# First sequence's norm taken on rows, its K in a second PSUM bank, passes for the clock, later transposes, and V's copies on ScalarE

## The chip, the cores and the metric

The kernel runs on one core of one Trainium2 chip. The metric is the device time in microseconds, as the median of several executions. The engines are PE (TensorE), DVE (VectorE), ACT (ScalarE), POOL (GpSimd) and SP (SyncE, which only issues transfers here). [...]

## What is computed

x has 4 sequences of 512 tokens and 128 channels, all in float32. Two blocks follow each other, each on a layer norm and with a residual:

```
x = x + attention(layernorm(x))     # 16 heads of 64, S = 512
x = x + six_layers(layernorm(x))    # depth 6, windows of 32
```

The first block, in which the whole change lies:

```
q, k, v = x @ Wq, x @ Wk, x @ Wv            # 128 -> 16 heads x 64
scores = q . k / 8 - 50 * (key after query)  # a penalty, not a mask
out = softmax(scores) @ v @ Wr
```

The layer norm has no weights here: `(x - mean) / sqrt(var + 1e-5)` over the 128 channels of a token. The second block has six layers of windowed attention with normalised and rotated q and k, and a gated feed-forward; the change does not touch it.

## The kernel before

**Staging.** The kernel has two stages. The first stage (about 0 to 560 us) computes the first block, the second (to the end) the six layers. The order of all instructions on every engine is written out by hand; each engine takes them in the order of the source, apart from some transfers on SP.

**Layout.** x is loaded per sequence as `xr[b]`, with tokens in the partitions (128 rows, 4 tiles of 128 channels). `load_x` (L196 to L201) transposes the four tiles on PE into one PSUM bank (`pt_bank`, two buffers), and ACT copies them to `x0T[b]`, channels in the partitions and the 512 tokens along the free axis. `xr` has two buffers, so sequences 2 and 3 are loaded into the tiles of 0 and 1 once those were read. `xnT[b]` is the normed sequence in the same layout as `x0T`.

**The norm** (`layernorm_steps`, three steps) works on the transposed layout. `mean` multiplies by a matrix of 1/128 on PE (L94), subtracts on DVE (L96) and squares on ACT (L98). `var` sums the squares with four small products (L103), and DVE, or POOL for the later sequences, takes the inverse root by three Newton steps of four instructions (`rsqrt`, L80 to L86). `scale` spreads the result over the partitions with four transposes (L111) and multiplies (L115). For sequence 0 the steps stand in front of everything, with the transposes of all four sequences between them:

```
load_x(0); mean(); load_x(1); var(); load_x(2); load_x(3); scale()
make_q(0, 0)(); make_k(0, 0)
```

**Slots.** The rest of the first stage is a loop of 64 slots m, each with two tiles of 128 queries for a pair of heads c of a sequence b: `b, c, odd = m // 16, m // 2 % 8, m % 2`. In a slot PE computes the scores of two tiles (`scores`, L252) and adds the penalty (L267), DVE takes the row maxima (`maximum`, L279, and L281 for the columns that are all penalised), ACT the exponents with their sums (L290), DVE the inverse sums (L300, L301), POOL multiplies by them (`normalise`, L304). The products of the slot before, `old`, are transposed by PE (L315) and copied out by ACT (L319) and DVE (L323). `times_v1` (L335) multiplies older ones with V. An even slot computes the next pair's Q (`make_q`, L215, copied by ACT at L217), an odd one its K (`make_k`, L221, copied by DVE at L223).

**V** is computed by `make_v` (L231), one tile of 128 tokens for 8 heads at a time, copied by DVE at L238. There are 32 such copies of 128x512: two in slot 0, three in slot 1, and one in most odd slots.

**Banks.** Q, K, V, the steps of the norm and the output projection all use one PSUM bank, `bank1` with one buffer: each of these products waits until the copy of the one before has read it. `tmp` and `small` are pools in SBUF.

**Order on DVE in a slot:** the maximum of the first tile with its bias (L279, L281), V's copy if there is one, a step of the next sequence's norm if there is one, the copy at L323, the maximum of the second tile, K's copy in odd slots, then the sums and the second L323.

**Transfers.** SP issues the x loads, the constants and the second stage's weights; ACT's queue issues Wq, Wk and Wv at the start.

## Time and profile before

| what | value |
|---|---|
| median of 3 runs | 2278.62 us (2278.29 to 2281.74) |
| profiled execution: its time, and its span | 2281.5 us, 2279.7 us |
| PE busy | 2178.0 us (96%), 35088 instructions |
| DVE busy | 1729.1 us (76%), 2800 instructions |
| ACT busy | 1347.6 us (59%), 2550 instructions |
| POOL busy | 1451.3 us (64%), 1981 instructions |
| start of the first score product | 26.97 us |
| V's copy on DVE (L238) | 32 of 0.68 us |
| a copy of the same shape on ACT (L319) | 128 of 0.59 us |

In a line of the timeline the first number is the start in us from the first instruction, the second how long the group took; then engine, line of the source, operation, output<-input with shapes, and the count. A bracket tells how long the engine stood idle before it and what released it. PE counts a float32 product as two instructions. PEld is PE's loading of weights, which overlaps its products. The granted clock is the share of TensorE's full clock.

### The profile page before, as it was taken

Reading aid. Unit: us, or ns where it says so; the run is one execution under the profiler, and the core shown is the slowest. Engines: PE = TensorE matmul, PEld = TensorE weight load, DVE = VectorE, ACT = ScalarE, POOL = GpSimd, SP = SyncE. Lnnn points to the kernel's source line nnn. Section 1 sums busy time; section 2 is a strip of 40 time slices with the busy share of each in tenths; the row PEclk is TensorE's granted clock in tenths of the full one; section 3 lists DMA queues with packets and bytes.
Section 4 is the critical chain, followed back from the end, with each engine's and each line's share of the span. In section 5 each row is a group of like instructions: output and inputs, shape, how many; then the busy total and the mean of one; then the engine's idle time right before and its main releaser. Section 6 shows DMA issues by size and latency. Waiting matters only on the chain.

```text
span 2279.7 us, 82205 instructions
## 1 busy us (share of the span) xinstructions
PE 2178.0 (96%) x35088; PEld 1435.6 (63%) x35088; DVE 1729.1 (76%) x2800; ACT 1347.6 (59%) x2550; POOL 1451.3 (64%) x1981
## 2 busy tenths in 40 slices
PE   6999999999999999999999999999999999999997
PEld 3555555555566666666666666666666666666664
DVE  3776667767778787878887788878888878888774
ACT  3665655655455656666566666666656666666562
POOL 1544545455877677767677777677776667766760
PEclk8999999999999999999999999999999999999998
DMA  3000000000322233232322323222332223222220
GB/s 115 1 1 1 1 1 1 1 1 1 75 70 64 63 88 75 58 75 68 87 67 64 77 70 91 64 62 69 85 85 56 72 63 88 73 67 70 65 56 15
DMA packets 91029, 125.74 MB, mean 55 GB/s; under 512 B 25390, under 2 KB 39468, under 8 KB 90668
## 3 DMA queue, kind: packets, MB, share of 16 engines
q1 hardware_dynamic: 90236, 118.92, 21.1%
q8 instruction: 279, 4.57, 0.9%
q10 hardware_dynamic: 432, 1.57, 0.2%
q14 instruction: 82, 0.67, 0.1%
HBM read 20.31 MB, written 1.05 MB: 9 GB/s over the span
## 4 chain that ended last, share of the span: by engine, by line
PE 63%; DVE 9%; issue 2%; ACT 1%; POOL 0%; POOLq 0%; ACTq 0%
PE ps_proj L477 19%; PE ps_one L585 14%; PE ps_one L680 7%; PE ps_att L655 6%; PE ps_att L623 6%; PE ps_proj L713 3%; PE ps_proj L714 3%; PE ps_proj L727 2%; DVE yt L80 2%; DVE t L502 1%; DVE rot L498 1%; PE ps_att L612 1%; PE ps_one L94 1%; PE ps_one L103 1%; DVE yt L83 1%
## 5 line engine op out<-in xcount | busy, mean ns | idle before, releaser
L513 POOL TENSOR_TENSOR rot<-rot,t 128x1024 f32<-128x1024 f32 x192 | 453.8, 2364 | 197.5 <-DVE t L502 185.9
L477 PE MATMUL ps_proj<-wqkv,xs 128*128 128x512 f32 x1152 | 553.3, 603 | 4.3 <-DVE t L502 2.8
L304 POOL TENSOR_TENSOR pr<-pr,den 128x1024 f32<-128x1024 f32 x128 | 240.9, 1893 | 266.9 <-DVE den L301 258.6
L488 ACT ACTIVATE sq<-ps_proj 128x1024 f32<-128x1024 f32 x192 | 196.8, 1025 | 356.7 <-PE ps_proj L477 324.5
L521 POOL TENSOR_TENSOR rot<-rot,ss 128x1024 f32<-128x1024 f32 x192 | 365.2, 1902 | 14.9
L477 PEld LDWEIGHTS ps_proj<-wqkv,xs 128*128 128x128 f32 x1152 | 198.1, 190 | 166.1 <-issue 146.5
L493 DVE TENSOR_REDUCE ss<-sq 128x16 f32<-128x1024 f32 x192 | 233.1, 1214 | 46.9 <-ACT sq L488 46.3
L498 DVE TENSOR_TENSOR rot<-ps_proj,lt 128x1024 f32<-128x1024 f32 x192 | 233.6, 1217 | 0.0
L502 DVE TENSOR_TENSOR t<-ps_proj,lt 128x1024 f32<-128x1024 f32 x192 | 233.2, 1215 | 0.4 <-POOL rot L513 0.4
L290 ACT ACTIVATE pr<-ps_sc,nm 128x128 f32<-128x128 f32 (+3 forms) x448 | 220.1, 507 | 20.0 <-DVE nm L279 16.7
L279 DVE TENSOR_REDUCE nm<-ps_sc 128x2 f32<-128x1024 f32 x128 | 156.0, 1219 | 91.0 <-PE ps_sc L267 91.0
L585 PE MATMUL ps_one<-ident,rot 128*128 128x128 f32 x1536 | 211.3, 280 | 5.9 <-issue 4.4
L680 PEld LDWEIGHTS ps_one<-aT,wo 128*128 128x128 f32 x1536 | 186.3, 192 | 45.3 <-issue 44.5
L83 POOL TENSOR_TENSOR yt<-y 128x32 f32<-128x32 f32 (+1 forms) x309 | 72.9, 236 | 210.5 <-DVE y L81 194.3
L633 DVE TENSOR_REDUCE mx<-ps_att 128x16 f32<-128x1024 f32 x96 | 117.5, 1224 | 102.3 <-PE ps_att L623 102.2
L680 PE MATMUL ps_one<-aT,wo 128*128 128x128 f32 x1536 | 187.3, 275 | 0.4 <-ACT aT L588 0.4
L585 PEld LDWEIGHTS ps_one<-ident,rot 128*128 128x128 f32 x1536 | 165.3, 141 | 25.3 <-issue 7.1
L319 ACT COPY pT<-ps_pt 128x512 f32<-128x512 f32 x128 | 75.5, 590 | 176.2 <-PE ps_pt L315 176.2
L655 PEld LDWEIGHTS ps_att<-vw,pT 64*32 64x32 f32 x9216 | 103.5, 105 | 93.4 <-ACT pT L588 54.0
L567 ACT COPY vt<-ps_proj 128x512 f32<-128x512 f32 x192 | 103.2, 590 | 93.6 <-PE ps_proj L477 91.6
L315 PEld LDWEIGHTS ps_pt<-ident,pr 128*128 128x128 f32 x1024 | 117.6, 142 | 56.7 <-issue 47.6
L655 PE MATMUL ps_att<-vw,pT 64*32 64x65 f32 x9216 | 129.0, 225 | 24.2 <-DVE t L502 13.4
(134 smaller groups left out, 4062.3 us busy)
## 6 DMA issues: line engine op xcount, KB each, us to landing
vw<-vt SPq DMA_DIRECT2D x1152, 65.0 KB
vw_first<-vt SPq DMA_DIRECT2D x336, 65.0 KB
wqkv<-in_wqkv_dram SPq DMA_DIRECT2D x18, 512.0 KB
wo<-in_wo_dram SPq DMA_DIRECT2D x6, 512.0 KB
w<-in_w_dram SPq DMA_DIRECT2D x6, 341.0 KB
xr<-in_x_dram SPq DMA_DIRECT2D x4, 256.0 KB
out_dram<-tmp_t SPq DMA_DIRECT2D x4, 256.0 KB
w<-in_w_dram SPq DMA_DIRECT2D x12, 64.0 KB
```

What stands on the lines that cost most here:

```text
L290: nc.scalar.activation(self.pr[:, h, cols], self.sc[:, h, cols], AF.Exp, bias=self.nm[:, part_, h : h + 1], accum_out=self.den[:, part_, h ...
L304: nc.gpsimd.tensor_tensor(self.pr, self.pr, self.den[:, 0].unsqueeze(2).to_broadcast([P, 2, S]), ALU.mult)
L477: mm(p[:, c, :], lhsT=u.xs[:, u.T * P : (u.T + 1) * P], rhs=wpart[j][:, c * 512 : (c + 1) * 512], start=True, stop=True,)
L488: nc.scalar.activation(u.sq, u.p[j], AF.Square)
L493: nc.vector.tensor_reduce(u.ss[:, j * HEADS : (j + 1) * HEADS], heads(u.sq), AX.X, ALU.add)
L498: nc.vector.tensor_tensor(heads(t0), heads(pf), lt[:, u.T, 2 * j].unsqueeze(1).to_broadcast([P, HEADS, HD]), ALU.mult)
L502: nc.vector.tensor_tensor(t1.rearrange("p (h t d) -> p h t d", t=2, d=half), pf.rearrange("p (h t d) -> p h t d", t=2, d=half)[:, :, ::-1, :],
L513: nc.gpsimd.tensor_tensor(u.r[j], u.r[j], u.t1, ALU.add)
L521: nc.gpsimd.tensor_tensor(heads(u.r[j]), heads(u.r[j]), u.ss[:, j * HEADS : (j + 1) * HEADS].unsqueeze(2).to_broadcast([P, HEADS, HD]), AL ...
L585: nc.tensor.transpose(tp[:, c * P : (c + 1) * P], src[:, (4 * g + c) * P : (4 * g + c + 1) * P], ident)
L655: mm(o[j * W : (j + 1) * W, h, c * (HD + 1) : (c + 1) * (HD + 1)], lhsT=u.pT[h * HD : (h + 1) * HD, 4 * g + c, j * W : (j + 1) * W], rhs=u ...
L680: mm(y[:, 0:P], lhsT=wo_w[0][:, c, :], rhs=u.aT[:, c, :], start=(c == 0), stop=(c == NC - 1))
```

## The change

The change has five parts.

- **x of sequence 0 in halves.** SP loads tiles 0 and 1, ACT's queue loads tiles 2 and 3, ahead of Wq, Wk and Wv.
- **First norm on rows.** `first_norm` replaces the three steps for sequence 0. DVE takes mean and variance of each token from `xr[0]` with `bn_stats` and `bn_aggr` (four each), adds eps, takes the inverse root as before, and scales the four tiles; each is then transposed by PE, and ACT copies the four to `xnT[0]`. `load_x(0)` remains, for the residual. Sequence 1's transposes stand between the statistics and the new transposes.
- **Passes for the clock.** `warm(n)` issues n products that nobody reads: ten of 128x128 at the very start, and sixteen of 24 columns between sequence 1's transposes and the new ones.
- **K's bank.** The first K goes to a bank of `pt_bank`, the first Q stays in `bank1`. `load_x(2)` and `load_x(3)` move to the end of slots 2 and 3.
- **V's copies on ACT**, all 32. With it the bias of the maxima is a method of its own (`bias`), and the first tile's stands after the norm step instead of ahead of it.

```diff
--- before.py
+++ after.py
@@ -174,8 +174,12 @@
         pen = s1.tile([P, P], BF16, tag="pen", name="pen")
         xr = [s1.tile([P, NT, EMB], F32, tag="xr", name=f"xr{b}", bufs=2) for b in range(B)]
         for b in range(B):
-            nc.sync.dma_start(out=xr[b], in_=x[b].rearrange("(t p) e -> p t e", p=P))
-            if b == 0:
+            src = x[b].rearrange("(t p) e -> p t e", p=P)
+            if b:
+                nc.sync.dma_start(out=xr[b], in_=src)
+            else:
+                nc.sync.dma_start(out=xr[b][:, 0:2], in_=src[:, 0:2])
+                nc.scalar.dma_start(out=xr[b][:, 2:NT], in_=src[:, 2:NT])
                 nc.sync.dma_start(out=ident16, in_=a["ident16"])
                 nc.sync.dma_start(out=pen, in_=a["pen"])
         for t_, n_ in ((wq, "wq"), (wk, "wk"), (wv, "wv")):
@@ -205,7 +209,38 @@
                 xnT[b] = s1.tile([P, S], F32, tag="xnT", name="xnT", bufs=2)
                 return xnT[b]
 
-            return layernorm_steps({}, bank1, lambda: x0T[b], out_, eng=nc.gpsimd if b else nc.vector)
+            return layernorm_steps({}, bank1, lambda: x0T[b], out_, eng=nc.gpsimd)
+
+        def warm(n, rhs=avg):
+
+            p = bank1()
+            for _ in range(n):
+                mm(p[:, 0 : rhs.shape[1]], lhsT=avg, rhs=rhs, start=True, stop=True)
+
+        def first_norm():
+
+            x_ = xr[0]
+            raw = small.tile([P, NT, 6], F32, tag="bnst", name="bnst", bufs=1)
+            mv = small.tile([P, NT, 2], F32, tag="bnmv", name="bnmv", bufs=1)
+            for t in range(NT):
+                nc.vector.bn_stats(raw[:, t, :], x_[:, t, :])
+            for t in range(NT):
+                nc.vector.bn_aggr(mv[:, t, :], raw[:, t, :])
+            rs = small.tile([P, NT], F32, tag="rs", name="rs")
+            nc.vector.tensor_scalar(rs, mv[:, :, 1], EPS, None, ALU.add)
+            load_x(1)
+            warm(16, raw.rearrange("p t k -> p (t k)"))
+            rsqrt(rs, NT, nc.vector)
+            h = tmpt()
+            tp = pt_bank()
+            for t in range(NT):
+                cols = slice(t * P, (t + 1) * P)
+                nc.vector.tensor_scalar(
+                    h[:, cols], x_[:, t, :], mv[:, t, 0:1], rs[:, t : t + 1], ALU.subtract, ALU.mult
+                )
+                nc.tensor.transpose(tp[:, cols], h[:, cols], ident)
+            xnT[0] = s1.tile([P, S], F32, tag="xnT", name="xnT", bufs=2)
+            nc.scalar.copy(xnT[0], tp)
 
 
         qs, ks, vs, pTs, os_, aTs = {}, {}, {}, {}, {}, {}
@@ -216,8 +251,8 @@
             q = qs[b, c] = s1.tile([P, S], F32, tag="q1", name="q1", bufs=2)
             return lambda: nc.scalar.activation(q, p, AF.Copy, scale=0.125)
 
-        def make_k(b, c):
-            p = bank1()
+        def make_k(b, c, p=None):
+            p = bank1() if p is None else p
             mm(p, lhsT=wk[:, c * P : (c + 1) * P], rhs=xnT[b], start=True, stop=True)
             k = ks[b, c] = s1.tile([P, S], F32, tag="k1", name="k1", bufs=2)
             nc.vector.tensor_copy(k, p)
@@ -235,7 +270,7 @@
                 start=True,
                 stop=True,
             )
-            nc.vector.tensor_copy(vs[b, j][:, t, :], p)
+            nc.scalar.copy(vs[b, j][:, t, :], p)
 
         class Rows:
 
@@ -277,6 +312,8 @@
                 sc = self.sc
                 self.nm = small.tile([P, 2, 2], F32, tag="nm", name="nm")
                 nc.vector.tensor_reduce(self.nm[:, 0], sc, AX.X, ALU.max, negate=True)
+
+            def bias(self):
                 if self.t + 1 < NT:
                     nc.vector.tensor_scalar(self.nm[:, 1], self.nm[:, 0], PEN, None, ALU.add)
 
@@ -353,16 +390,11 @@
 
         rows = [Rows(b, c, t) for b in range(B) for c in range(NC) for t in range(NT)]
         norms, norms1 = {}, {}
-        mean, var, scale = norm_x(0)
+        warm(10)
         load_x(0)
-        mean()
-        load_x(1)
-        var()
-        load_x(2)
-        load_x(3)
-        scale()
+        first_norm()
         make_q(0, 0)()
-        make_k(0, 0)
+        make_k(0, 0, pt_bank())
 
 
         last = len(rows) // 2
@@ -392,11 +424,14 @@
                 norms[b + 1][c - 1]()
             if b in range(1, B) and not odd and 4 <= c <= 6:
                 norms1[b - 1][c - 4]()
+            if now:
+                now[0].bias()
             if old:
                 old[0].transposes()
             if now:
                 now[0].exponents()
                 now[1].maximum()
+                now[1].bias()
 
             bn, cn = (b, c + 1) if c + 1 < NC else (b + 1, 0)
             copies = []
@@ -411,6 +446,8 @@
                 now[1].exponents()
             for f in copies:
                 f()
+            if m in (2, 3):
+                load_x(m)
             if now:
                 now[1].inverse()
                 now[1].normalise()
```

## Prediction

> **What bounds the kernel now.** I read the page first: PE is busy 96% of the span, and the chain that ended last is 63% PE. The change touches only the first stage (0 to 560 us) and its start, so the answers must come from the first microseconds, then from one repeating slot.

> First the timeline of the start, up to the first score matmul:

> ```profile
> 5.64 1.08 PE L199 MATMUL ps_pt<-ident,xr 128*128 128x128 f32 x4 [5.64 <-DMA xr<-in_x_dram]
> ...
> 7.40 2.07 PE L94 MATMUL ps_pj<-x0T,avg 128*128 128x512 f32 x2 [0.68 <-ACT x0T L201]
> ...
> 9.29 1.11 PE L199 MATMUL ps_pt<-ident,xr 128*128 128x128 f32 x4
> ...
> 14.79 0.16 DVE L86 TENSOR_TENSOR rs<-y,yt 128x4 f32<-128x4 f32 x1
> ...
> 15.96 1.09 PE L199 MATMUL ps_pt<-ident,xr 128*128 128x128 f32 x4 [3.99 <-DMA xr<-in_x_dram]
> ...
> 18.64 1.08 PE L199 MATMUL ps_pt<-ident,xr 128*128 128x128 f32 x4 [1.60 <-DMA xr<-in_x_dram]
> ...
> 19.52 1.06 PE L111 MATMUL ps_pj<-ident,rs 128*128 128x128 f32 x4
> ...
> 21.36 2.07 PE L215 MATMUL ps_pj<-xnT,wq 128*128 128x512 f32 x2 [0.78 <-DVE xnT L115]
> ...
> 24.11 2.08 PE L221 MATMUL ps_pj<-xnT,wk 128*128 128x512 f32 x2 [0.69 <-ACT q L217]
> ...
> 26.97 3.79 PE L252 MATMUL ps_sc<-k,q 64*128 64x256 f32 x16 [0.78 <-DVE k L223]
> ```

> The reader is to see that the inverse root is ready at 14.95, but PE, which works in order, stands behind the transposes of sequences 2 and 3 until 19.4: 4.4 us that the norm doesn't need. Q and K share one bank, so K's matmul waits for Q's copy. The first scores start at 26.97. Each 128x512 product takes 2.07 us here. Next, stretches of the same time; the columns after the stretch are PE, PEld, DVE, ACT and POOL busy, granted clock, DMA share and GB/s:

> ```profile
> 7.30:10.70 3.40, 3.01 (x6) 1.22 (x6) 0.69 (x1) 0.52 (x2) 0.00 (x0) 1.00 1.06 378
> 10.70:14.10 3.40, 1.05 (x8) 0.97 (x8) 1.75 (x11) 0.63 (x2) 0.00 (x0) 1.00 1.09 348
> 14.10:17.50 3.40, 1.09 (x4) 0.71 (x4) 0.71 (x5) 0.42 (x1) 0.00 (x0) 0.50 1.13 312
> ...
> 24.30:27.80 3.50, 2.72 (x6) 1.06 (x8) 0.69 (x1) 0.00 (x0) 0.00 (x0) 0.50 0.00 0
> 27.80:31.20 3.40, 3.40 (x19) 2.32 (x18) 0.08 (x1) 0.00 (x0) 0.00 (x0) 0.50 0.00 0
> 31.20:34.60 3.40, 2.14 (x5) 0.48 (x4) 2.15 (x4) 1.93 (x8) 0.00 (x0) 1.00 0.00 0
> ```

> The granted clock is half until 31.2, except 10.7 to 14.1. A stretch with PE busy 3.01 of 3.40 raised it, one of 2.72 did not, one of 1.05 dropped it. (The 1.00 before 10.7 is only a missing record: the 2.07 us product at 7.40 ran at half clock.)

> Then one odd slot of the steady part (its first score matmul at 164.09, the next slot's at 172.21):

> ```profile
> 166.26 1.08 PE L231 MATMUL ps_pj<-wv,xnT 128*128 128x512 f32 x2
> 166.34 1.22 DVE L279 TENSOR_REDUCE nm<-ps_sc 128x2 f32<-128x1024 f32 x1 [0.20 <-PE ps_sc L267]
> ...
> 167.68 0.68 DVE L238 COPY v<-ps_pj 128x512 f32<-128x512 f32 x1
> 167.81 0.59 ACT L319 COPY pT<-ps_pt 128x512 f32<-128x512 f32 x1 [2.08 <-PE ps_pt L315]
> ...
> 168.42 1.13 PE L221 MATMUL ps_pj<-xnT,wk 128*128 128x512 f32 x2 [0.21 <-DVE v L238]
> ```

> V's product ends at 167.34, but DVE is in the maximum until 167.56, so V's copy ends at 168.36, and K's product, which needs the same single bank, waits. ACT stood idle for 2.08 us up to 167.81. The waits of PE between 40 and 555 us say how often:

> ```profile
> PE ps_pj L221 <- DVE v L238: 8.5, 27, 0.6
> ```

> It is the largest of PE's waits in the stage. A plain slot without V takes 6.78 us (539.36 to 546.14); with V's product, 1.0 more, it should take 7.8. The odd slots take 8.12 to 8.48.

> [...] 2.07 against 1.08 us for the same product, and its changes lie multiples of 3.4 us apart. [...] Here they seem to count: without the 1.11 us of transposes at 9.29 the stretch that raised the clock held under 2.1 us, less than the 2.72 that did not. [...] From 3.0 to 3.5 us ACT's queue (q10, weights) and SP's (q1, x) stood so:

> ```profile
> q10 hardware_dynamic: 40, 0.16, 83.4%
> q1 hardware_dynamic: 45, 0.02, 15.2%
> ```

> Turns are about equal in number, so x in small packets gets a ninth of the bytes.

> **The change part by part.** The first sequence's path:

> - *Load in halves.* Half of x's packets no longer stand behind the other half, and ACT's half goes ahead of Wq. Landing at about 4.2 instead of 5.64 (estimate: 512 packets took from 1.8 to 5.0 here, 256 in each of two queues should be through by 3.5, plus the 0.65 seen between last packet and use). ACT's issues grow by one of 0.45, and Wv's issue waits for it: Wv is needed only at 20. SP's third x load now waits for the new norm's last read (about 10) and stands ahead of wr, the tables and W1/W2: none is read in the first 48 us, so nothing.
> - *Norm on rows.* It removes L94, L96, L98, L103, the four broadcast transposes L111 and L115. It adds on DVE four statistics and four aggregations (not in this trace; nearest rows: 0.16 for tiny ones, 0.68 for 128x512, so 0.15 to 0.35 each, I take 0.2), the same root (12.00 to 14.95, 2.95), four scalings at 0.25. From 4.2: 1.6 + 2.95 + 1.0 gives 9.8. This is **not** the path.
> - *Unread passes.* The first ten are 20 instructions at 0.26 (half of a 2.07/2 for a quarter of the columns), 1.05 to 6.3: they delay the first transposes, whose product is read only at the first residual. The other sixteen are 32 instructions of 24 columns, and they stand behind sequence 1's transposes, which waited for their data until 9.29. Those packets still fight the weights, so I leave 9.3, then 1.1. For the tiny passes the nearest row is L103 (1.00 us for 8 at full clock): 4.0 us; at half clock double, 8.0. I take 5.0, since PE is busy from 9.3 and the clock may rise underway. So PE reaches the new norm's transposes at 15.4, not at 9.8: the passes and the wait for sequence 1 are the path.
> - *On to the scores.* Transposes 0.8, ACT copy with its latency 0.7, Q 1.1, K at once in its own bank 1.1, DVE copy 0.75: scores at 19.9 instead of 26.97. **Gain 7.1** (9 if the clock is kept up and 4.0 holds; 2 if the clock stays at half, with Q and K at 2.07).

> The first two slots. Before, 26.97 to 48.24, 21.3 us. After: scores at full clock 2.0 instead of 3.79; V's copies on ACT right after each product, which puts the exponents 5.9 behind the slot's start (before 5.4); three V products of 1.1 with copies of 0.6 between them in the second slot, as now. Stepping through gives 19.3. **Gain 2.0** (0 to 3).

> *Later transposes.* Sequences 2 and 3 go into slots 2 and 3, behind the last transposes. Four at 0.13 are 0.5 us; but each takes the bank that DVE's copy of the slot's last transposes frees. In slot 2 that copy ends at 56.89, and the next scores started at 57.70 with their second row: 0.75 lost. In slot 3 it ends at 64.44, while PE was free for the next product at 63.3: it waits 1.1, works 0.5, and the next scores come 1.8 later. **Loss 2.6** (0.5 to 3.5). ACT's two extra copies of 0.58 fall into its idle time.

> *V's copy on ACT.* The product ends at 167.34, ACT is idle, the copy ends at 168.0, and K's product can start when PE's transposes end, about 168.2. Gained: the wait, and the 0.1 by which the product after it is shorter when it needn't start anew (1.02 against 1.13): 0.32 in slots of 8.12, up to 0.65 in the slower ones, where DVE was later still; over 27 slots **9.5** (6 to 12). What is queued behind it on ACT: the pT copy and the exponents move back 0.2 us. POOL's normalising then ends 0.2 later, and its reader in the next slot had 1.6 us to spare (173.0 against 174.6). The shifted bias lets L96 and L115 start 0.08 earlier in 12 norm slots that PE waits for: **0.7**.

> The second stage is the same program, started earlier; its weights were in by 20 us. Nothing there.

> Sum: 7.1 + 2.0 - 2.6 + 9.5 + 0.7 = 16.7. The profiled execution took 2281.5 (span 2279.7 and 1.8 around it), so 2264.8 of that kind; it lies 2.9 above the median of 2278.62, so **2262** as a median. A measurement here can tell about 0.2% (4.6 us) from no change.

> **Rivals.**

> - *Prologue without profit:* tiny passes don't hold the clock, or cost 8 us. The first scores come at 24 to 25 at half clock: 2 + 0 - 2.6 + 10.2 = 9.6 gained, 2269. For it: no run shows what tiny passes do to the clock. Against: PE is without a gap from 9.3 on.
> - *The stall moves:* in the slots another wait (scores for the exponents, transposes for POOL) takes the place of V's. Then 6.5 from the start alone, 2272. For it: POOL ends waits in the last slots (0.73 and 1.06 us at 550 to 554). Against: slots of 6.78 run with the same chain.
> - *Slower: V's copy on ACT comes late.* If ACT still has exponents of the slot before when V's product is done, V's copy waits, K's product behind it, and every exponent moves back 0.59: 28 x 0.59 = 16.5 lost and no 9.5 gained; with 6.5 from the start 10 slower, 2289. It decides once the 2.08 us of idle ahead of L319 are gone.
> - *Better still:* sequence 1 lands by 7 and the added transposes hide: 2255.

> **How the numbers follow.** Forecast 0.62, prologue 0.15, stall moves 0.13, slower 0.05, better 0.05. Range 2254 to 2274: from "better" to just past "stall moves"; it leaves out the slower case and the tails. Faster by over 0.2% (below 2274.0): nearly all but the slower case and a part of the second rival, 0.89; within 0.06; slower 0.05.

> **What would show it.** First score matmul at 19.9 (18 to 21 right, over 23 wrong); the sixteen passes 4 to 6 us; scores of slot 2 some 19 us after the first; odd slots near 7.8; no wait of K's product for V; a wait of the added transposes for DVE's pT copy in slot 3. Odd slots still at 8.1, or new POOL waits there, would make it wrong.

## The result, and the profile after

| | before | after |
|---|---|---|
| median, runs on the same chip | 2280.53 us (6 runs, 2278.29 to 2281.91) | 2265.16 us (6 runs, 2263.34 to 2271.15) |
| ratio | | 0.9937 [0.9924, 0.995] |
| profiled execution: time, span | 2281.5, 2279.7 us | 2271.15, 2269.1 us |

The kernel is 15.4 us faster. The forecast was 16.7 us, so the total was right. The terms of which it was summed were not all right. The profiled execution of after is the slowest of its six, so its span shows less gain (10.6 us) than the medians do. One execution in this document, the profiled one of best_cold (4045.73 us), was disturbed and is left out.

Busy time on the page of after shows the copies of V moved from DVE (1729.1 us before) to ACT (1347.6 before), and PE, the bound, as busy as it was:

```profile
PE 2179.3 (96%) x35130; PEld 1443.3 (64%) x35130; DVE 1709.7 (75%) x2778; ACT 1361.3 (60%) x2582; POOL 1453.4 (64%) x1981
```

Next the timeline of the start, in the columns used before:

```profile
1.06 4.64 PE L218 MATMUL ps_pj<-avg 128*128 128x128 f32 x20 [1.06 <-DVE hsel L61]
3.51 0.87 DVE L226 BATCH_NORM_STATS2 bnst<-xr 128x6 f32<-128x128 f32 x4 [2.26 <-DMA xr<-in_x_dram]
...
9.67 0.66 PE L203 MATMUL ps_pt<-ident,xr 128*128 128x128 f32 x4 [3.11 <-DMA xr<-in_x_dram]
10.16 6.55 PE L218 MATMUL ps_pj<-bnst,avg 128*128 128x24 f32 x32
16.54 1.09 PE L241 MATMUL ps_pt<-ident,tmp_t 128*128 128x128 f32 x4
18.31 2.07 PE L250 MATMUL ps_pj<-xnT,wq 128*128 128x512 f32 x2 [0.68 <-ACT xnT L243]
20.18 1.91 PE L256 MATMUL ps_pt<-xnT,wk 128*128 128x512 f32 x2
22.96 3.79 PE L287 MATMUL ps_sc<-k,q 64*128 64x256 f32 x16 [0.88 <-DVE k L258]
```

The first statistics start at 3.51, and the scaled tiles are ready at 8.80. PE comes to their transposes only at 16.54: it waited 3.11 us for sequence 1's data, and then worked through the unread passes for 6.55 us. K follows Q at once. The first scores start at 22.96, but Q (2.07 us), K (1.91) and the scores (3.79) each take almost twice what they take at a granted clock of 1.00 (1.13, 1.02 and 2.00 in the profile of wide16, below). The stretches of that time (columns as before: PE, PEld, DVE, ACT, POOL busy, granted clock, DMA share, GB/s) show the clock they had:

```profile
7.10:10.50 3.40, 0.83 (x8) 0.84 (x8) 1.59 (x7) 0.21 (x2) 0.00 (x0) 1.00 0.98 375
10.50:13.90 3.40, 3.40 (x18) 3.40 (x17) 0.00 (x0) 0.45 (x1) 0.00 (x0) 0.50 1.05 377
13.90:17.30 3.40, 3.40 (x18) 3.33 (x17) 0.00 (x0) 0.00 (x0) 0.00 (x0) 0.50 1.16 286
```

Behind the ten passes of 128 columns and the transposes that follow them (busy 2.85 of 3.40 from 3.7 to 7.1) the clock was full: 1.00 from 7.1 to 10.5, and four transposes took 0.66 us at 9.67, against 1.06 at 5.49. The wait for sequence 1 left PE busy 0.83 of 3.40 us, and the clock fell to 0.50. Then the narrow passes filled the next stretch and most of the one after it (the norm's transposes filled the rest), without a gap, and the clock stayed at half. It stayed there for 17.1 us in all, from 10.5 to 27.6. In the traces of before and after every change of the clock lies 3.4 us or a multiple of it behind the one ahead of it (here 3.4 us at full, then 17.1 at half; in before 3.4 from 10.7, then 17.1 from 14.1), and the stretches of 3.4 us in this document follow these steps.

In the repeating part, an odd slot (first score matmul at 158.46, the next slot's at 166.18):

```profile
160.63 1.08 PE L266 MATMUL ps_pj<-wv,xnT 128*128 128x512 f32 x2
160.72 1.23 DVE L314 TENSOR_REDUCE nm<-ps_sc 128x2 f32<-128x1024 f32 x1 [0.15 <-PE ps_sc L302]
...
161.74 0.59 ACT L273 COPY v<-ps_pj 128x512 f32<-128x512 f32 x1 [1.65 <-PE ps_pj L266]
...
162.41 1.09 PE L256 MATMUL ps_pj<-xnT,wk 128*128 128x512 f32 x2
```

ACT takes V 0.03 us after the product, while DVE is in the maximum until 161.95, and K's product no longer has a bracket of idle time. The slot takes 7.72 us. In the waits of PE between 40 and 545 us the group of 8.5 us for V is gone. The largest is now the added transposes:

```profile
PE ps_pt L203 <- DVE pT L360: 3.6, 2, 2.0
```

Last, the border of the two stages: two stretches of after, and then the first projections of before (first fence) and of after (second):

```profile
539.60:543.00 3.40, 2.57 (x9) 1.86 (x9) 0.69 (x1) 0.59 (x1) 0.00 (x0) 0.50 0.00 0
543.00:546.40 3.40, 3.40 (x6) 0.97 (x6) 0.00 (x0) 0.30 (x1) 0.00 (x0) 0.50 0.02 5
```

```profile
558.10:603.50 45.40, 41.65 (x527) 21.08 (x527) 31.02 (x37) 16.55 (x25) 30.09 (x51) 1.00 0.24 58
```

```profile
542.20:589.60 47.40, 43.58 (x526) 21.47 (x526) 31.03 (x37) 16.56 (x25) 30.00 (x51) 0.96 0.24 57
```

The same 36 projections take 45.4 us before and 47.4 after, where two half-clock windows (stretches of 3.4 us at half clock, 539.6 to 546.4) lie across the start of the latter (a third came later, 624.9 to 628.3). PE's work and the other engines' are otherwise the same.

The distances between first score matmuls give the terms of the sum in the two profiled executions:

| term | forecast | measured |
|---|---|---|
| first score matmul, 26.97 to 22.96 | 7.1 | 4.0 |
| slots 0 and 1, 21.27 to 21.03 | 2.0 | 0.2 |
| slots 2 and 3, 16.88 to 18.69 | -2.6 (without V) | -1.8 |
| other slots, to the first projection | 9.5 + 0.7 | 13.4 |
| second stage | 0 | -5.3 |
| sum, against the span | 16.7 | 10.6 |

Up to the first projection after is 15.9 us ahead (542.19 against 558.05); then it loses a third of that.

### The profile page after: what moved, and what is told of

Read it like the earlier page. It is cut to its first block, busy times and chain, and to the rows that moved or that the text cites. A ratio compares the mean times of both kernels' runs of the same rounds, so it can differ in the third digit from the quotient of the medians.

```text
span 2269.1 us, 82300 instructions
## 1 busy us (share of the span) xinstructions
PE 2179.3 (96%) x35130; PEld 1443.3 (64%) x35130; DVE 1709.7 (75%) x2778; ACT 1361.3 (60%) x2582; POOL 1453.4 (64%) x1981
## 3 DMA queue, kind: packets, MB, share of 16 engines
q1 hardware_dynamic: 89980, 118.79, 21.3%
HBM read 20.31 MB, written 1.05 MB: 9 GB/s over the span
## 4 chain that ended last, share of the span: by engine, by line
PE 64%; DVE 9%; issue 2%; ACT 1%; POOL 0%; ACTq 0%; POOLq 0%
PE ps_proj L514 19%; PE ps_one L622 13%; PE ps_one L717 7%; PE ps_att L692 6%; PE ps_att L660 6%; PE ps_proj L750 3%; PE ps_proj L751 3%; PE ps_proj L764 3%; DVE yt L80 2%; DVE t L539 1%; DVE rot L535 1%; PE ps_att L649 1%; PE ps_one L94 1%; PE ps_one L103 1%; DVE y L81 1%
## 5 line engine op out<-in xcount | busy, mean ns | idle before, releaser
L530 DVE TENSOR_REDUCE ss<-sq 128x16 f32<-128x1024 f32 x192 | 233.1, 1214 | 49.5 <-ACT sq L525 48.8
L701 DVE RECIPROCAL rden<-ps_att 128x8 f32<-128x8 f32 x192 | 38.9, 203 | 145.0 <-PE ps_att L692 144.9
```

The costliest lines, as they stand in the source:

```text
L530: nc.vector.tensor_reduce(u.ss[:, j * HEADS : (j + 1) * HEADS], heads(u.sq), AX.X, ALU.add)
```

## The experiments

In every experiment the ratio is to before, run on the same chip in the same comparison. Kernels of different comparisons are set beside each other by that ratio, not by their microseconds.

**Are the narrow passes to blame for the half clock?** `wide16` gives the sixteen passes 128 columns in place of 24, `no16` takes them out, and `x1_late` takes them out and moves sequence 1's transposes, for whose data PE waited, behind the first K.

```diff
 # wide16, against after
-            warm(16, raw.rearrange("p t k -> p (t k)"))
+            warm(16)
 # no16
-            warm(16, raw.rearrange("p t k -> p (t k)"))
 # x1_late
-            load_x(1)
-            warm(16, raw.rearrange("p t k -> p (t k)"))
 ...
         make_k(0, 0, pt_bank())
+        load_x(1)
```

> The changed kernel with the sixteen unread passes 128 columns wide instead of 24, nothing else. Theory: passes of 24 columns keep PE occupied (0.205 us each of 32) but do not count as busy for the clock, so Q, K and the first scores run at half clock; wide ones count. Then the clock is full from about 14 us, the passes end near 16, the first scores start at about 20 and take 2.0 us instead of 3.79; some 4 to 5 us faster than the changed kernel, about 2261. Rival: the width does not matter and the clock was low because of where its windows fell; then 32 passes at 0.26 take 8.3 us, the first scores start near 24.7 and still take 3.8, about 2 us slower than the changed kernel.

The median was 2267.79, ratio 0.9925 [0.9913, 0.9937]. The timeline of its start, and the two stretches around the change of the clock:

```profile
9.31 5.01 PE L218 MATMUL ps_pj<-avg 128*128 128x128 f32 x32
...
18.30 2.00 PE L287 MATMUL ps_sc<-k,q 64*128 64x256 f32 x16 [0.88 <-DVE k L258]
```

```profile
8.60:12.00 3.40, 3.40 (x17) 3.40 (x18) 0.21 (x1) 0.58 (x1) 0.00 (x0) 0.50 1.03 417
12.00:15.40 3.40, 2.77 (x25) 2.53 (x23) 0.00 (x0) 0.58 (x1) 0.00 (x0) 1.00 1.15 313
```

Behind one stretch full of 128-column work (transposes up to 9.31, then the passes) the clock was 1.00, behind after's stretch from 10.5 to 13.9, full of 24-column passes alone, it was 0.50 (busy 3.40 of 3.40 in both). Four more profiles with the narrow passes also stayed at half behind them (Q took 2.07 us in after_again and k_bank1, K 1.91 in x23_slot0, and in v_back the half clock lasted up to 26.1). So the same busy share stood ahead of the full clock in wide16 and of the half clock in after. That the width makes the difference is not shown: the operand differs too (a constant in place of the statistics), and no run separates the two. The first scores start 4.7 us sooner than in after (up to 1.2 of it because sequence 1's transposes, which wait for their data, started at 8.47 and not at 9.67), and the first projection, at 536.97, 5.2 sooner. At the end of the two profiled executions 3.2 are left, and the ratios overlap, so a gain of that size in the total is neither shown nor excluded. A part went back in a half-clock window from 46.1 to 49.5, in which the scores of slot 3 took 3.59 us (2.00 in after), and the slot 11.58 (9.93 in after). Ahead of it stands the stall that the moved transposes brought:

```profile
42.70:46.10 3.40, 1.37 (x12) 0.97 (x12) 1.50 (x5) 3.40 (x16) 1.28 (x1) 1.00 0.01 2
46.10:49.50 3.40, 3.40 (x18) 2.28 (x17) 0.80 (x2) 1.35 (x3) 2.51 (x2) 0.50 0.01 2
```

PE, waiting 2.03 us for DVE's pT copy, was busy 1.37 of that stretch, and the clock of the next one was 0.50. After has the same wait of 2.03 us in slot 2, but there it lies across two stretches, busy 2.02 (48.1 to 51.5) and 2.73 (51.5 to 54.9), and the clock stayed at 1.00. So a half-clock window followed the same wait in one of the two profiles, the one in which the wait lay within one stretch.

> The changed kernel without the sixteen unread passes. Theory: they stand on the path from sequence 1's transposes to the first norm's transposes and give nothing back; the first scores start at about 16.5 instead of 22.96, at half clock as now: about 6 us faster than the changed kernel, near 2259. Rival: in most executions the passes do hold the clock, and the profiled one was an exception; then leaving them out saves 4 to 6 us and loses 4 to 5 of clock, no difference of more than 2 us.

2259.91, ratio 0.99 [0.9887, 0.9913]: faster than after, the intervals don't meet. From its timeline:

```profile
10.70 2.07 PE L249 MATMUL ps_pj<-xnT,wq 128*128 128x512 f32 x2 [0.68 <-ACT xnT L242]
...
15.28 2.00 PE L286 MATMUL ps_sc<-k,q 64*128 64x256 f32 x16 [0.88 <-DVE k L257]
```

The first scores come 7.7 us sooner than in after (up to 1.6 of it from sequence 1's data, whose transposes started at 8.06), and at full clock, where half clock was expected: Q and K themselves, at half clock (2.07 and 1.83 us), kept PE busy for 3.40 of 3.40 us from 10.8 to 14.2, and from 14.2 on the clock was 1.00. Slot 0 takes 7.55 us (9.75 in after). Between these two profiles the sixteen passes are therefore a pure loss, in PE's time (6.55 us in after) and in the clock (first scores of 3.79 us in after, 2.00 here).

> The changed kernel without the sixteen passes and with sequence 1's transposes behind the first K instead of ahead of the first norm's transposes. Theory: PE then no longer waits for sequence 1's data (landed at 9.6); the norm's transposes start with the first scaled tile at about 8, the first scores at about 14.5, half clock: 8 us faster than the changed kernel, near 2257. Rival: the scaled tiles were late anyhow, or Wq and Wk land only by then; first scores at 16.5, no better than without the passes alone.

2261.5, ratio 0.9906 [0.9893, 0.9918], not to be told from no16. The first scores start at 14.50, only 0.8 sooner than in no16. There sequence 1's transposes had started at 8.06 and the norm's at 8.96; here the norm's started at 7.93, so the move could bring 1.0 at most, and Q and K still ran at half clock (2.07 and 1.91 us). Slot 3 took 11.44 us, again with a half-clock window (41.9 to 45.3, scores of 3.50 us) behind the wait of the added transposes (2.03 us). The size expected was too large.

The two kernels also part at the border of the stages. Their last slots run alike, product for product, up to the drop of the clock; only the stretches of 3.4 us fall differently on the slot's gaps (first line no16, second x1_late):

```profile
526.20:529.60 3.40, 1.41 (x11) 0.93 (x10) 0.86 (x2) 1.42 (x4) 3.27 (x2) 1.00 0.00 0
526.60:530.00 3.40, 1.82 (x12) 0.86 (x8) 0.91 (x3) 1.90 (x6) 3.39 (x2) 1.00 0.00 0
```

The first begins 6.6 us after the last slot's first score matmul, and half clock follows it (529.6 to 536.4). The second begins 6.1 us after it, and the clock stays full (mean from 530 to 570: 0.92 in no16, 1.00 in x1_late).

**What do V's copies bring, and what the shifted bias?** `v_only` is before with V's copies on ACT and nothing else; `v_back` is after with V's copies on DVE again, the bias still shifted.

```diff
 # v_only, against before; v_back is the same edit of after, the other way round
-            nc.vector.tensor_copy(vs[b, j][:, t, :], p)
+            nc.scalar.copy(vs[b, j][:, t, :], p)
```

> The kernel before with V's 32 copies on ACT, nothing else. Theory: odd slots of 8.12 to 8.48 become about 7.7 to 7.8 and PE's wait of K's product for V goes; 9 to 10 us faster than before, near 2270. Rival: the gain in the slots comes from the bias behind the norm step and from the earlier start, and another wait takes the place of V's; then less than 4 us.

2271.52, ratio 0.9962 [0.9947, 0.9976]. Odd slots take 7.71 us (8.12 to 8.48 before), the even slots with a step of the norm still 8.12. The first projection starts 12.0 us sooner, and the second stage takes what it took before (1721.96 against 1721.66). Slot 3 took 10.24 us (9.23 before), with a half-clock window (57.2 to 60.6) behind a stretch that was busy 1.74 of 3.40: no transposes are added there, so this window came without theirs.

> The changed kernel with V's 32 copies back on DVE. Theory: the odd slots go back to 8.12 and more, the wait of K's product for V comes back, and about 9.5 us of the gain go: near 2274. Rival: the shifted bias alone lets V's copy follow the maximum sooner; then less than half of it goes.

2269.91, ratio 0.9946 [0.9933, 0.996]. Odd slots take 7.93, not 8.12, and the norm slots 7.92. So with V on DVE the shifted bias alone takes 0.19 off an odd slot, since it lets V's copy follow the maximum directly; with V on ACT it adds nothing there (7.71 with and without it). It takes 0.20 off each norm slot. The two edits overlap: from slot 4 to the first projection V's copies alone (v_only) bring 11.9 us, the shifted bias alone (v_back) 9.4, both together (after) 13.4, after losing 0.8 us of that to half clock in the last slot (eight transposes of 1.91 us there, 1.09 before). So undoing one cost less than was expected, and the total of v_back cannot be told from after's.

**What does the place of the moved transposes cost?** `x23_slot0` puts both into slot 0, where the first exponents haven't come yet and no transposed products stand in the banks.

```diff
-            if m in (2, 3):
-                load_x(m)
+            if m == 0:
+                load_x(2)
+                load_x(3)
```

> The changed kernel with the transposes of sequences 2 and 3 both at the end of slot 0, where both banks are free and PE waits for the exponents, instead of at the ends of slots 2 and 3. Theory: the two waits of 2.0 and 1.6 us for DVE's pT copy go, slot 2 is back at 7.7, slot 3 at 8.5 or less: 2 to 3 us faster than the changed kernel. Rival: the data of sequence 3 land too late or ACT's two copies push back slot 1; then slots 0 and 1 grow by as much.

2261.05, ratio 0.9911 [0.9895, 0.9926]. In its timeline the eight transposes run without a wait, behind Q's product:

```profile
29.06 1.04 PE L203 MATMUL ps_pt<-ident,xr 128*128 128x128 f32 x8
```

Slots 2 and 3 take 7.11 and 8.68 us (8.76 and 9.93 in after), together 2.9 less. The interval of the ratio overlaps after's by a little (0.9924 to 0.9926), so the total alone does not show the gain. Slot 0 is also 2.1 shorter, but its first scores ran at full clock in this execution (2.00 us, 3.79 in after), before the edited place; that part isn't the edit's.

**All of it together.** `best` is after with sequence 1's transposes behind the first K, the other two in slot 0, and six passes of 128 columns in place of the sixteen narrow ones. `best_cold` is the same without any pass.

```diff
 # best, against after; best_cold has neither warm(6) nor warm(10)
-            load_x(1)
-            warm(16, raw.rearrange("p t k -> p (t k)"))
+            warm(6)
 ...
         make_k(0, 0, pt_bank())
+        load_x(1)
 ...
-            if m in (2, 3):
-                load_x(m)
+            if m == 0:
+                load_x(2)
+                load_x(3)
```

> The changed kernel with sequence 1's transposes behind the first K, six passes of 128 columns in place of the sixteen of 24 (behind sequence 0's transposes, while DVE is at the inverse root), and sequences 2 and 3 at the end of slot 0. Theory: the first scores start at 12.5 to 13 at full clock, slots 2 and 3 lose their waits: 3 to 5 us faster than with sequence 1 late alone, near 2257. Rival: the clock drops at the gap before Q all the same, or the passes delay the norm's transposes; first scores at 14.5 or later, and only the slots' 2 to 3 us remain.

2248.19, ratio 0.9853 [0.984, 0.9867]: the lowest ratio of all, clear of those of after and x1_late, and below the 2257 expected. From its timeline:

```profile
5.56 1.50 PE L218 MATMUL ps_pj<-avg 128*128 128x128 f32 x12
8.14 1.10 PE L240 MATMUL ps_pt<-ident,tmp_t 128*128 128x128 f32 x4 [1.08 <-DVE tmp_t L237]
...
12.78 2.00 PE L286 MATMUL ps_sc<-k,q 64*128 64x256 f32 x16 [0.44 <-DVE k L257]
```

Now PE waits for DVE's norm (1.08 us), and not the norm for PE: first scores at 12.78, at full clock (2.00 us). The granted clock is 1.00 from 4.7 us to 2189 without a break, and the lead of 32.0 us at the first projection is kept to the end. Over x1_late it is 6.3 us ahead there: 1.7 from the start, 4.5 from slots 2 and 3 (where x1_late had a half-clock window). The other 3.3 in the spans come in the second stage, whose program is the same.

> The kernel of the run best (sequence 1 behind the first K, sequences 2 and 3 in slot 0) without any unread pass, neither the ten nor the six. Theory: the clock is half until Q, K and the transposes have filled a window, so Q and K take 2.07 us each; the first scores start at about 14.5 instead of 12.78, and the first ones may run at half clock too (3.79 instead of 2.0): 2 to 4 us slower than best, near 2251. Rival: the order alone makes the gain, and the passes give nothing that a measurement can tell.

Its other three executions took 2253.03 to 2254.01, ratio 0.9868 [0.985, 0.9887]. That is 0.0015 above best, or 3.4 us, but the intervals overlap: what passes of full width bring by themselves is not settled, and no profile of it can be read.

**Two smaller ones.** `k_bank1` puts the first K back into Q's bank; `after_again` is after, unaltered.

```diff
 # k_bank1
-        make_k(0, 0, pt_bank())
+        make_k(0, 0)
```

> The changed kernel with the first K back in the single bank that Q uses. Theory: K's product waits for Q's copy on ACT, 0.6 to 0.7 us; the first scores start 0.7 to 0.9 later after Q's start than in the changed kernel (4.65 there). Rival: Q's copy was hidden; no difference.

One execution, 2274.32. K's product waits again for Q's copy (0.69 us). From Q's start to the scores it took 5.62 us, against 4.65 in after: the second bank is worth 0.97 us there. The total, a single time, carries no verdict.

> The changed kernel itself, unaltered, beside best_cold on one chip, for the spread of its runs. Theory: the half-clock windows fall differently in each execution, so the start of the second stage and its first layer vary: a profile with another set of half-clock windows, a span between 2260 and 2270, and the same ratio of about 0.994. Rival: the two half-clock windows at 540 and 625 us belong to the kernel and come again.

2267.69, ratio 0.9933 [0.9917, 0.9948]. Half-clock windows stood again at 536.3 to 543.1 and 621.6 to 625.0, so they are no accident of one execution; that they come in every one is not shown. The start differs: sequence 1's data came 1.4 us sooner, the passes took 5.16 us, and the scores started at 20.20 instead of 22.96, still at half clock:

```profile
20.20 3.79 PE L287 MATMUL ps_sc<-k,q 64*128 64x256 f32 x16 [0.88 <-DVE k L258]
```

## Why the prediction was right, and where it was wrong

**The direction and the size of the total held** because the largest term, V's copies, was read from a slot that repeats: a wait that ends on a busy DVE, 27 times, with an idle ACT beside it. v_only shows it by itself, 12.0 us at the first projection. That the sum came out so close is luck in part, as the end of this section says.

- *Load in halves and the norm's path: right.* The halves were put at 4.2, and the first statistics ran at 3.51. Statistics took 0.22 each, aggregations 0.09 (0.15 to 0.35 was allowed for both) and scalings 0.28 (0.25); the tiles were ready at 8.80 (forecast 9.8) and weren't the path.
- *The sixteen passes: the step that failed.* "I take 5.0, since PE is busy from 9.3 and the clock may rise underway." PE was busy, as said (3.40 of 3.40 us from 10.5 to 13.9), and the clock did not rise: it was 0.50 behind that stretch, and 1.00 behind one as busy in wide16. The row they were priced by, L103 (1.05 us for eight, not 1.00), stood in a stretch that was busy 1.05 of 3.40, so it could not tell what such products do when they fill one. The passes took 6.55 us in the profile (5.16 in after_again; by estimate 1.4 us of them ran at full clock there, since 32 at 0.205 us would make 6.6), and Q, K and the scores ran at half clock. This was the mechanism of the rival "prologue without profit", and its start (first scores at 24 to 25) lies nearer the profile's 22.96 than the forecast's 19.9. The start brought 4.0 instead of 7.1, and a part of that is this execution's: in v_back, x23_slot0 and after_again, where the start is the same program, sequence 1's transposes began 1.1 to 1.4 sooner, and the scores at 22.27, 22.38 and 20.20. The 20.20 lies inside the 18 to 21 that the forecast called right, but at half clock: there the number agreed and the mechanism did not.
- *The first two slots: wrong for the same reason.* The forecast of 2.0 rested on first scores of 2.0 us; they took 3.79. no16, with 2.00, has a slot 0 shorter by 2.2.
- *Later transposes: right in mechanism and size.* Both wait for DVE's pT copy, 2.03 and 1.56 us. Slots 2 and 3 grew by 1.8 in sum with V's gain in slot 3 included, and x23_slot0 gives 2.9 back. What was missed: in wide16 and x1_late such a wait of 2.03 us fell within one stretch of 3.4 us (42.7 to 46.1 and 38.5 to 41.9), half clock followed (0.50 for 3.4 us), and slot 3 took another 1.5 to 1.7 us. It was not the added wait alone: v_only had a half-clock window in slot 3 without it (57.2 to 60.6).
- *V's copies and the bias: right in mechanism, too small in size.* Odd slots were forecast at 7.8 and took 7.71, since K's product started 3.95 us into the slot, before the recorded end of the transposes for which the forecast let it wait (4.1). No wait of K for V is left, and PE's waits for POOL grew only from 2.1 to 2.7 us, so the rivals "the stall moves" and "slower" fell. The other slots brought 13.4 instead of 10.2. The part for the bias was mis-sized most: 0.20 in each of 11 norm slots, 2.2 in all, where 0.08 in 12 was put (which makes 0.96, not the 0.7 of the sum). And the forecast took the two edits as independent: the bias alone brings 9.4 us, because it also lets V's copy on DVE start 0.20 sooner, so V's copies on ACT add only about 4 to it.
- *"Nothing there" in the second stage: wrong in the profile.* The program there is the same, but it starts at another moment, and half-clock windows fell on its first projections. They came in both profiles of after. They also came at that border in wide16, no16, x23_slot0 and k_bank1, and not in before, v_only, v_back, x1_late and best. The cost is 2 to 2.6 us in the first 36 projections. The profiles with and without them differ in where the stretches of 3.4 us fall on the last slot. In the eleven that can be read the slot's work up to there is the same but for 0.2 us in before. Half clock followed in all six where a stretch began 6.4 to 7.0 us after the slot's first score matmul, and in none of the five where none began between 6.2 and 7.2 (the nearest are x1_late's at 6.1 and before's at 7.3). What sets that position, and how often each kernel meets it, stays open. The windows are not all of it either: after was 5.0 behind some 94 us into the stage, where its third window had passed, but v_back's second stage took 5.8 us longer than before's with no half-clock window from 26.1 to 2152.6. Why the stage varies so is not shown.

The errors nearly cancelled in the total, which is luck: the start and first slots fell short by 4.9 us, the repeating slots and the transposes gave 4.0 more. The median of 2265.16 lies 3.2 above the forecast. The windows at the border (2 to 2.6 us) would be most of that if they came in most executions, which two profiles cannot show.

## What to carry to other kernels

Judge a pass that is to hold the clock by the clock behind it, not by the engine's busy share: with 3.40 of 3.40 us busy it was 1.00 behind passes of 128 columns (wide16) and 0.50 behind those of 24 (after), which cost 6.55 us of PE as well. Whether even the wide ones pay is open, as best and best_cold cannot be told apart. An engine that takes its work in order should get late data late: for the data of sequence 1 and for the pT bank PE waited 3.11 and 2.03 us, and the transposes themselves took 0.66 each time. And a copy belongs on the engine that is idle when its product ends (here ACT, idle for 2.08 us, while DVE was in a maximum of 1.22): find that in the slot that repeats, and multiply it by the slots. Before moving it, see what stands ahead of it on its own engine: here one small instruction moved out of its way brought most of the same gain (9.4 of 11.9 us).
